# Sixteen expert blocks run inside the end of the first stage, on a row table read from the sort's sum of the first eight pairs

## Chip, core and metric

The kernel runs on one core of a Trainium2 chip. The metric is the device time of one launch in microseconds (us): 733.31 is the median of three runs of the kernel before (730.54 to 735.48).

## What is computed

`x` holds 32 sequences of 56 tokens of width 256; each sequence has a context of 1500 rows. Four steps follow one another, each added to the residual. The second one concerns the change: a mixture of 16 experts in which every token takes the 6 with the highest scores. The code below is shortened.

```python
x = x + xattn0(layernorm(x), ctx, ...)   # a decayed scan over ctx, averaged over its 1500 rows, then a norm
x = x + moe0(layernorm(x), ...)          # 16 experts, the best 6 per token
x = x + xattn1(layernorm(x), ctx, mask)  # softmax attention over the unmasked rows
x = x + moe1(layernorm(x), ...)          # 2 experts, the best 1

def moe0(h, gate_w, w_gate, w_up, w_down):          # h: 1792 x 256
    scores = softmax(h @ gate_w.T)                  # 1792 x 16
    topk_w, topk_idx = top_k(scores, 6)
    cw = zeros(1792, 16).at[rows, topk_idx].add(topk_w)
    y = 0
    for e in range(16):
        out = silu(h @ w_gate[e].T) * (h @ w_up[e].T) @ w_down[e].T   # inner width 176
        y = y + cw[:, e:e + 1] * out
    return y
```

## The kernel before

**Pairs.** Two sequences share one tile of 128 partitions, so there are 16 pairs (`NP`). PE, DVE, ACT and SP follow the order of the program as written (L90) throughout; POOL does so from the second stage on.

**First stage** (L234 to L767). A loop over the pairs (L643) streams the context through a ring of five slots of 1.5 MB (`slots`, `load_ctx`), sums it on TensorE (`count_in`, acc L325), forms the first residual, norms it (`first_norm`, `residual`, `second_norm`), writes the normed rows to DRAM (`away`, `xn0`) and scores the experts (`gate`, `best`). The pairs are staggered over the steps of the loop: pair p is normed one step after it is summed, ranked two after and sorted three after.

**Sorting tokens to experts.** `ranks` and `counted` give each chosen token its place in the queue of its expert (`pos`; `base0` is the running count). `places` splits this place into a level (place divided by 128, at most 14) and an offset. `ones_at` builds one-hot rows of the offsets, half of one of its two tiles on POOL. `sorted_in` (owned L593) multiplies and sums them into one PSUM bank, `owned`: for each expert and level, the 128 token numbers and their weights. It is summed over all 16 pairs in one go. A block is one level of one expert: 128 rows; the blocks are ordered by level, so that blocks 0 to 15 are the first 128 rows of each expert.

**The tail of the first stage** (L685 to L767) finishes pairs 13, 14 and 15, copies `owned` to SBUF, and picks out the rows of the used blocks (bl L750) into `idx` (row numbers), `wgt` (weights) and `ei` (which expert each block has). `busy` (d L583) issues matmuls on data that nothing reads. The weights of the 16 experts (`w0_sb`) come over SP's queue: the down weights in pieces (`w0_down_pieces`), the up weights at pair 13 (`load_w0_up`).

**Second stage**: `expert_blocks` over 95 blocks (`NB0`), written out in steps. In step t, TensorE does the gate and up product of block t (`gate_up`, gu L785), turns the hidden rows of block t-1 (`turn`, tp L803), turns the gathered rows of block t+1 (tp L195, copied by ACT L197) and does the down product of block t-2 (`down`, y L812). ACT applies silu (sg L791), DVE the product (hs L797). POOL gathers each block's rows by `idx` (xb L943), seven blocks ahead; the result goes to DRAM (`ys0`). `side(t)` hangs other work on step t: the windows of context for the third stage (`load_window`), the residual written out (`xr0`), the mask rows, and the gathers that add finished blocks back to the residual (`result`, L856).

**Third and fourth stage**: the attention, and the two experts over 15 blocks. After them a general path runs only if the flag `bad` is set (L1439).

Of the kernel before, what the change touches and what calls it, by code (L numbers as in the profile page):

```python
# [8 lines left out]
F32 = mybir.dt.float32  # L9
# [34 lines left out]
NB0 = NBW - E0 // 4  # L44
NY1 = 3
NB1 = B * S // P + 1
WP = 2 * D + 2
# [12 lines left out]
def xattn_ffn_kernel(  # L60
# [91 lines left out]
    starts = const.tile([1, B], I32, name="starts")  # L152
    bad = const.tile([1, 1], I32, name="bad")

    ring = const.tile([P, NRING, CW], F32, name="ring")
# [78 lines left out]
    with tc.tile_pool(name="p1", bufs=1) as p1, tc.tile_pool(name="p3", bufs=3) as p3, tc.tile_pool(  # L234
# [19 lines left out]
        bin_sb = p1.tile([P, KD], F32, name="bin_sb")  # L254
        bout_sb = p1.tile([1, D], F32, name="bout_sb")
        gam = p1.tile([P, D], F32, name="gam")
# [110 lines left out]
        PE.matmul(vp[:, 0:D], lhsT=ones[0:1, :], rhs=bout_sb, start=False, stop=True)  # L367
        cvec = p1.tile([1, D], F32, name="cvec")
        A.copy(cvec, vp[0:1, 0:D])
# [16 lines left out]
        for l in range(NL):  # L386
            G.memset(lev[:, l, :], float(l * P))
        iota = p1.tile([P, P], F32, name="iota")
# [189 lines left out]

        def busy(n):

            for _ in range(n):
                d = psa.tile([P, 512], F32, tag="acc", name="d")
                PE.matmul(  # L583
                    d, lhsT=ident, rhs=slots[B % NRING][:, 0:2, :].rearrange("p j d -> p (j d)"),
                    start=True, stop=True,
                )

        def sorted_in(p, h=None):

            t = pend[p]  # L590
            for e in range(E0) if h is None else range(NE * h, NE * h + NE):
                c, g = divmod(e, 4)
                PE.matmul(  # L593
                    owned[Q * g : Q * g + Q, c, :],
                    lhsT=vals[:, p % 2, e].rearrange("p o l -> p (o l)"),
                    rhs=t["hots"][e // NE][:, e % NE, :],
                    start=(p == 0 and c == 0), stop=(p == NP - 1 and c == 3),
                )
# [44 lines left out]
        for p in range(NP):  # L643
            if p >= 1:
                first_norm(p - 1)
            if p >= 3:
                ones_at(p - 3, 0)
            if p >= 1:
                residual(p - 1)
                count_in(2 * p)  # L650
                count_in(2 * p + 1)
            sum_out(p)
            if p >= 1:
                second_root(p - 1)
# [24 lines left out]
            if p % 2 == 0 and p + 2 < NP:  # L679
                first_rows(p + 2)  # L680
            if p == NP - 3:
                load_w0_up()
            if p > NP - 3:
                some_pieces(6)
        last = NP - 1  # L685
# [24 lines left out]

# [14 lines left out]
        for c in range(4):  # L725
# [43 lines left out]
    def expert_blocks(nb, nq, f, w, ei, wk, ptr, pgu, pht, py, rows_of, done, ahead, wgt=None, side=None, xT0=None):  # L769

# [3 lines left out]
        piece = doff + 2 * D  # L774
        units = [(i, u) for i in range(nb) for u in range(nq)]
        xT, at, hs, hT, y = {}, {}, {}, {}, {}
# [42 lines left out]

        xb = {i: rows_of(i) for i in range(min(ahead, nb))}  # L820
        xT[0] = xT0 or turned_rows(wk, ptr, "tr", xb[0])
        xb.pop(0)
        if side:
            side(-1)
        for t in range(len(units) + 2):
# [11 lines left out]
            if side:  # L837
                side(t)

# [88 lines left out]
    with tc.manual_schedule(  # L928
# [82 lines left out]
        def late_or_bad():  # L1011
# [7 lines left out]
            V.tensor_reduce(t8s[0:1, 0, 0:1], lp[0:1, 0:P], AX.X, ALU.max)  # L1019
            V.tensor_scalar(bad, t8s[0:1, 0, 0:1], 0.0, bad, ALU.is_gt, ALU.max)  # L1020
            V.tensor_scalar(
                bad, slot[0:1, NL - 1, E0 - 1 : E0], float(NB0), bad, ALU.is_gt, ALU.max
            )

        todo = [(blocks_by(p) + 4, p, k) for p in soon for k in range(K0)]
        sums = []
# [12 lines left out]
        def side(t):  # L1039
# [5 lines left out]
            if t > 1:  # L1045
                for _ in range(3):
                    if ways_:
                        next_ = ways_.pop(0)
                        next_()
            if 0 < t <= B // 2:  # L1050
                load_window(t - 1)
            if t == B // 2 + 1:
                nc.sync.dma_start(
                    out=xr0.rearrange("(p r) d -> r p d", r=P), in_=xr,
                )
            if 0 < t - B // 2 - 1 <= B:
                b = t - B // 2 - 2
# [33 lines left out]
            NB0, 1, F0, w0_sb.rearrange("p e w -> p (e w)"), ei,  # L1091
            wk, ptr, pgu, pht, py, rows_of, done, 7, wgt, side,
        )
# [590 lines left out]
```

## Time and profile before

The profiled execution took 731.96 us; its span, from the first to the last instruction, is 730.3 us with a mean granted TensorE clock of 0.954.

| stretch, us from the start of the span | what runs there |
|---|---|
| 0 to 186 | the loop over the pairs; a pair each 8.5 to 9.2 us at its end |
| 186 to 214 | the tail of the first stage, up to the first gate and up product |
| 214 to 464 | the 95 expert blocks |
| 464 to 559 | the attention |
| 559 to 730 | the last mixture |

| engine | busy us | share of the span |
|---|---|---|
| PE | 655.7 | 90% |
| DVE | 401.3 | 55% |
| ACT | 241.5 | 33% |
| POOL | 349.5 | 48% |

A busy share is an average over stages with different limits; the chain of waits, which is followed back from the last instruction, tells which engine an interval was waiting for. PEld is the load of a matmul's stationary operand, which runs beside PE; the granted clock is a share of TensorE's full speed.

### The profile page before, as it was taken

The page shows a single profiled execution, that of the slowest core. Times are in us where ns is not written, and L with a number is a line of the kernel's source. Part 1 is how long each engine was busy: PE and PEld are TensorE (multiplying, and loading weights), DVE is VectorE, ACT ScalarE, POOL GpSimd, SP SyncE. Part 2 cuts the span into 40 slices and gives each one's busy share as a digit, 9 for nine tenths or more (in the row PEclk, how much of TensorE's full clock was granted, in tenths as well). Part 3 has the DMA queues.
Part 4 walks back from the last instruction along what each step waited for, and adds up shares of the span by engine and source line. Part 5 has one row for each costly group of instructions (what it writes and reads, how often), then busy time and mean ns, then how long its engine had stood idle before and what let it go on. Part 6 is the DMA issues. An engine that isn't in the chain of part 4 may idle for free.

```text
span 730.3 us, 13508 instructions
## 1 busy us (share of the span) xinstructions
PE 655.7 (90%) x4099; PEld 438.6 (60%) x4099; DVE 401.3 (55%) x1378; ACT 241.5 (33%) x704; POOL 349.5 (48%) x440
## 2 busy tenths in 40 slices
PE   3558988888779999999999999999988999999996
PEld 3424555555447777667777776666654666666664
DVE  3578687878824655534454447677876232322322
ACT  0113233333214444444444443566551111111110
POOL 6265455554344357667776776568342202112111
PEclk9869799999669999999999999999999999999999
DMA  8969899999716899645554554695941201011000
GB/s 259 316 271 391 316 364 356 369 358 315 214 50 203 265 334 286 206 138 144 153 155 136 157 160 131 185 313 108 332 149 53 69 9 44 25 36 39 26 30 18
DMA packets 70656, 136.62 MB, mean 187 GB/s; under 512 B 7731, under 2 KB 43204, under 8 KB 70580
## 3 DMA queue, kind: packets, MB, share of 16 engines
q1 hardware_dynamic: 56036, 100.31, 39.9%
q0 software_dynamic: 14544, 35.37, 18.0%
q8 instruction: 38, 0.62, 0.4%
q14 instruction: 38, 0.31, 0.1%
HBM read 109.54 MB, written 26.77 MB: 187 GB/s over the span
## 4 chain that ended last, share of the span: by engine, by line
PE 77%; DVE 11%; ACT 3%; POOL 2%; issue 2%; DMA 1%; POOLq 0%; DVEq 0%
PE gu L785 29%; PE y L812 18%; PE acc L325 7%; PE tp L803 5%; PE tp L195 4%; PE tp L913 2%; PE sp L1142 2%; PE owned L593 2%; PE bp L467 1%; PE op L1177 1%; PE lp L505 1%; POOL xn L491 1%; PE sT L459 1%; DVE st L183 1%; ACT xT L197 1%
## 5 line engine op out<-in xcount | busy, mean ns | idle before, releaser
L785 PE MATMUL gu<-w_sb,xT 128*128 x380 | 130.8, 466 | 3.4 <-ACT xT L197 1.9
L791 ACT ACTIVATE sg<-gu 128x176 f32<-128x176 f32 (+1 forms) x155 | 53.1, 343 | 230.3 <-PE gu L785 227.9
L943 POOL DMA_INDIRECT xb<-xn,idx x95 | 91.2, 960 | 63.1 <-PE tp L195 39.7
L785 PE MATMUL gu<-ring,xT 128*128 x240 | 113.7, 597 | 0.0
L797 DVE SCALAR_TENSOR_TENSOR hs<-sg,wgt,gu 128x176 f32<-128x176 f32 x95 | 37.7, 397 | 119.8 <-ACT sg L791 119.8
L812 PE MATMUL y<-w_sb,hT 88*128 x380 | 97.9, 380 | 0.0
L785 PEld LDWEIGHTS gu<-w_sb,xT 128*128 128x128 f32 x380 | 71.5, 191 | 30.7 <-ACT xT L197 2.9
L856 POOL DMA_INDIRECT g<-ys,early x78 | 74.8, 959 | 29.1 <-issue 15.3
L795 DVE TENSOR_TENSOR hs<-sg,gu 128x256 f32<-128x256 f32 x60 | 25.2, 421 | 112.3 <-ACT sg L791 112.3
L1428 POOL DMA_INDIRECT out<-ob,ti x15 | 14.8, 989 | 126.8 <-DVE ob L1425 126.5
L803 PEld LDWEIGHTS tp<-ident,hs 128*88 128x88 f32 (+1 forms) x310 | 40.0, 129 | 57.9 <-issue 46.9
L812 PEld LDWEIGHTS y<-w_sb,hT 88*128 88x128 f32 x380 | 64.5, 190 | 5.7 <-issue 0.6
L785 PEld LDWEIGHTS gu<-ring,xT 128*128 128x128 f32 x240 | 45.6, 192 | 33.3 <-issue 30.4
L805 DVE COPY hT<-tp 88x256 f32<-88x256 f32 (+1 forms) x155 | 64.3, 415 | 0.2 <-PE tp L803 0.2
L812 PE MATMUL y<-ring,hT 128*128 x240 | 61.7, 380 | 0.0
L197 ACT COPY xT<-tp 128x256 f32<-128x256 f32 x126 | 46.9, 372 | 43.4 <-PE tp L195 35.3
L803 PE MATMUL tp<-ident,hs 128*88 128x128 f32 (+1 forms) x310 | 59.2, 273 | 0.0
L325 PE MATMUL acc<-ring,cz 128*32 128x256 f32 x768 | 54.7, 442 | 0.2 <-DVE cz L301 0.2
L951 ACT COPY yb<-y 128x256 f32<-128x256 f32 x95 | 35.3, 372 | 42.8 <-PE y L812 41.9
L432 POOL TENSOR_SCALAR z<-xr,mva,rsa 128x256 f32<-128x256 f32 x16 | 23.0, 1437 | 49.6 <-DVE xr L479 45.4
L195 PE MATMUL tp<-ident,xb 128*128 128x128 f32 x220 | 42.5, 275 | 2.4 <-issue 2.4
L812 PEld LDWEIGHTS y<-ring,hT 128*128 128x128 f32 x240 | 41.0, 190 | 3.3
(307 smaller groups left out, 996.7 us busy)
## 6 DMA issues: line engine op xcount, KB each, us to landing
ring<-in_cx SPq DMA_DIRECT2D x32, 1536.0 KB
ys<-yb SPq DMA_DIRECT2D x95, 128.0 KB
ring<-in_cx SPq DMA_DIRECT2D x16, 384.0 KB
extra<-in_cx SPq DMA_DIRECT2D x16, 384.0 KB
xs<-zrow SPq DMA_DIRECT2D x5, 771.0 KB
w_sb<-in_wg SPq DMA_DIRECT2D x2, 1408.0 KB
w_sb<-in_wu SPq DMA_DIRECT2D x2, 1408.0 KB
xn<-xn SPq DMA_DIRECT2D x16, 128.0 KB
```

The lines of the kernel that those rows point to most:

```text
L195: PE.transpose(tp[:, k * P : (k + 1) * P], xn[:, k * P : (k + 1) * P], ident)
L197: A.copy(xT.rearrange("p k c -> p (k c)"), tp[:, 0 : KD * P])
L325: PE.matmul(acc[Q * g : Q * g + Q, 0:D], lhsT=cz[:, j, 1 - h : 1 - h + Q], rhs=c[:, j, :], start=(h == 0 and m == 0), stop=(h == 1 and m = ...
L785: PE.matmul(gu[:, 0 : 2 * fp], lhsT=xT[i][:, k, :], rhs=w[:, bass.ds(at[i] + (u * piece + k * 2 * fp), 2 * fp)], start=(k == 0), stop=(k = ...
L791: A.activation(sg, gu[:, 0:fp], AF.Silu)
L797: V.scalar_tensor_tensor(hs[i, u], sg, wgt[:, i : i + 1], up, ALU.mult, ALU.mult)
L803: PE.transpose(tp[0:h, c * P : (c + 1) * P], a[:, c * h : (c + 1) * h], ident)
L805: V.tensor_copy(hT[i, u], tp[0:h, 0 : 2 * P])
L812: PE.matmul(y[i][:, 0:D], lhsT=a[:, c * P : (c + 1) * P], rhs=w[0:h, bass.ds(at[i] + (u * piece + doff + c * D), D)], start=(u == 0 and c ...
L856: G.indirect_dma_start(out=g, out_offset=None, in_=ys0[0 : n * P, :], in_offset=bass.IndirectOffsetOnAxis(ap=at[:, p, k : k + 1], axis=0),)
L943: G.indirect_dma_start(out=xb, out_offset=None, in_=xn0, in_offset=bass.IndirectOffsetOnAxis(ap=idx[:, i : i + 1], axis=0),)
L951: A.copy(yb, y[:, 0:D])
```

## The change

The sort's sum is cut in two: `owned` is summed over pairs 0 to 7, copied to `own0`, and started anew for pairs 8 to 15; at the end the two are added. From the first sum, `first_table` reads the first 128 rows of each expert, as row numbers `idx0` and weights `wgt0`. `soon_step` and its helpers run blocks 0 to 15 on these in 18 steps, placed among the instructions of the tail; the rows and results lie in ring slots that are free by then. The second stage starts at block 16. `busy` is taken out. If an expert had fewer than 128 rows after eight pairs and got more later, `lack` is positive and sets the flag `bad`. The windows, which go into the same ring slots, are loaded two per step in steps 16 to 23, and the residual is written out before block 16. The experts' up weights come in three parts. Copies by ACT stand in `soon_step` where `turn` uses DVE.

```diff
+PC = 8
...
-    def load_w0_up():
+    def load_w0_up(a, b):
         for m, w in ((0, wg0), (1, wu0)):
             for k in range(KD):
                 nc.sync.dma_start(
-                    out=w0_sb[:, :, (2 * k + m) * F0 : (2 * k + m + 1) * F0],
-                    in_=w[:, k, :].rearrange("p (e f) -> p e f", f=F0),
+                    out=w0_sb[:, a:b, (2 * k + m) * F0 : (2 * k + m + 1) * F0],
+                    in_=w[:, k, a * F0 : b * F0].rearrange("p (e f) -> p e f", f=F0),
                 )
...
+        def first_table():
+            V.tensor_scalar(cut, base0[0:1, :], float(P), None, ALU.min)
+            A.copy(own0.rearrange("p c r -> p (c r)"), owned.rearrange("p c r -> p (c r)"))
+            bl = ps.tile([P, 512], F32, tag="ps", name="bl")
+            for o in range(2):
+                for c in range(4):
+                    PE.matmul(
+                        bl[:, o * E0 + 4 * c : o * E0 + 4 * c + 4], lhsT=own0[:, c, :],
+                        rhs=ident.rearrange("p (g o l) -> p o l g", o=2, l=NLP)[:, o, 0, :],
+                        start=True, stop=True,
+                    )
+            V.tensor_copy(idx0, bl[:, 0:E0])
+            V.tensor_copy(wgt0, bl[:, E0 : 2 * E0])
...
-                    start=(p == 0 and c == 0), stop=(p == NP - 1 and c == 3),
+                    start=(p in (0, PC) and c == 0), stop=(p in (PC - 1, NP - 1) and c == 3),
...
                 sorted_in(p - 3)
+            if p - 3 == PC - 1:
+                first_table()
...
             if p == NP - 3:
-                load_w0_up()
+                load_w0_up(0, 4)
+                load_w0_up(4, 12)
             if p > NP - 3:
                 some_pieces(6)
+            if p == NP - 1:
+                some_pieces(len(pieces))
+                load_w0_up(12, E0)
...
+        def soon_rows(n):
+            for _ in range(n):
+                i = len(egot)
+                if i < E0:
+                    egot.append(i)
+                    G.indirect_dma_start(
+                        out=xbs[i], out_offset=None, in_=xn0[0 : PC * P, :],
+                        in_offset=bass.IndirectOffsetOnAxis(ap=idx0[:, i : i + 1], axis=0),
+                    )
...
+        def soon_turned(i):
+            tp = ps.tile([P, 512], F32, tag="ps", name="tp")
+            for k in range(KD):
+                PE.transpose(tp[:, k * P : (k + 1) * P], xbs[i][:, k * P : (k + 1) * P], ident)
...
+            A.copy(exT[i].rearrange("p k c -> p (k c)"), tp[:, 0:D])
+
+        def soon_step():
+            t = eat[0]
+            eat[0] += 1
+            if 0 <= t - 1 < E0:
...
+                A.activation(sg, gu[:, 0:F0], AF.Silu)
...
+                V.scalar_tensor_tensor(
+                    ehs[i], sg, wgt0[:, i : i + 1], gu[:, F0 : 2 * F0], ALU.mult, ALU.mult
+                )
+            if t < E0:
...
+                for k in range(KD):
+                    PE.matmul(
+                        egu[t][:, 0 : 2 * F0], lhsT=xT[:, k, :],
+                        rhs=w0_sb[:, t, 2 * k * F0 : 2 * (k + 1) * F0],
+                        start=(k == 0), stop=(k == KD - 1),
+                    )
+            if 0 <= t - 1 < E0:
...
+                for c in range(2):
+                    PE.transpose(tp[0:H0, c * P : (c + 1) * P], a[:, c * H0 : (c + 1) * H0], ident)
+                ehT[t - 1] = two_of("hT", D, D)[0:H0]
+                A.copy(ehT[t - 1], tp[0:H0, 0 : 2 * P])
+            if t + 1 < E0:
+                soon_turned(t + 1)
+            if 0 <= t - 2 < E0:
...
+                for c in range(2):
+                    o = 2 * KD * F0 + c * D
+                    PE.matmul(
+                        y[:, 0:D], lhsT=a[:, c * P : (c + 1) * P], rhs=w0_sb[0:H0, i, o : o + D],
+                        start=(c == 0), stop=(c == 1),
+                    )
+                yb = ybs[i % 8]
+                A.copy(yb, y[:, 0:D])
+                nc.sync.dma_start(out=ys0[i * P : (i + 1) * P, :], in_=yb)
+
         last = NP - 1
+        soon_rows(2)
         first_norm(last)
+        soon_turned(0)
         ones_at(NP - 3, 0)
         residual(last)
+        soon_rows(2)
         ones_at(NP - 3, 1)
         second_root(last)
         ranks(NP - 2)
         second_norm(last)
         away(last)
-        some_pieces(len(pieces))
+        soon_step()
+        soon_rows(2)
         sorted_in(NP - 3, 0)
         turned(last)
         sorted_in(NP - 3, 1)
         gate(last)
-        busy(1)
+        soon_step()
+        soon_rows(2)
         counted(NP - 2)
         places(NP - 2)
         best(last)
+        soon_step()
+        soon_rows(2)
         ranks(last)
         for h in range(2):
             ones_at(NP - 2, h)
+        soon_step()
+        soon_rows(2)
         for h in range(2):
             sorted_in(NP - 2, h)
         counted(last)
+        V.scalar_tensor_tensor(
+            lack, base0[0:1, :], float(P), cut, ALU.min, ALU.subtract
+        )
...
-        busy(1)
+        soon_step()
+        soon_rows(4)
         places(last)
         for h in range(2):
             ones_at(last, h)
+            soon_step()
...
+        soon_step()
         for h in range(2):
             sorted_in(last, h)
-        A.copy(own.rearrange("p c r -> p (c r)"), owned.rearrange("p c r -> p (c r)"))
+        V.tensor_tensor(own, owned, own0, ALU.add)
+        soon_step()
         bl = ps.tile([P, 512], F32, tag="ps", name="bl")
...
-        busy(2)
...
         V.tensor_copy(ei, ep[0:1, 0:P])
+        while eat[0] < E0 + 2:
+            soon_step()
...
-            if 0 < t <= B // 2:
-                load_window(t - 1)
-            if t == B // 2 + 1:
+            if t == E0 - 1:
                 nc.sync.dma_start(
                     out=xr0.rearrange("(p r) d -> r p d", r=P), in_=xr,
                 )
+            if 0 <= t - E0 < B // 4:
+                for h in range(2):
+                    load_window(2 * (t - E0) + h)
...
-        todo = [(blocks_by(p) + 4, p, k) for p in soon for k in range(K0)]
+        todo = [(max(blocks_by(p) + 4, E0 + 8), p, k) for p in soon for k in range(K0)]
```

More of the change, by code (lines that the diff above doesn't have):

```diff
@@ L153, in xattn_ffn_kernel @@
     bad = const.tile([1, 1], I32, name="bad")
+    lack = const.tile([1, E0], F32, name="lack")
     ring = const.tile([P, NRING, CW], F32, name="ring")
@@ L254, in xattn_ffn_kernel @@
         bin_sb = p1.tile([P, KD], F32, name="bin_sb")
-        bout_sb = p1.tile([1, D], F32, name="bout_sb")
+        bout_sb = pw0.tile([1, D], F32, name="bout_sb")
         gam = p1.tile([P, D], F32, name="gam")
@@ L367, in xattn_ffn_kernel @@
         PE.matmul(vp[:, 0:D], lhsT=ones[0:1, :], rhs=bout_sb, start=False, stop=True)
-        cvec = p1.tile([1, D], F32, name="cvec")
+        cvec = pw0.tile([1, D], F32, name="cvec")
         A.copy(cvec, vp[0:1, 0:D])
@@ L386, in xattn_ffn_kernel @@
         for l in range(NL):
-            G.memset(lev[:, l, :], float(l * P))
+            G.memset(lev[:, l, :], float(l * P) if l else -1.0)
         iota = p1.tile([P, P], F32, name="iota")
@@ L577, in ones_at @@
             pend[p].setdefault("hots", []).append(oh)
[L579 to L586, printed above, removed]
+        idx0 = p1.tile([P, E0], I32, name="idx0")
+        wgt0 = p1.tile([P, E0], F32, name="wgt0")
+        cut = p1.tile([1, E0], F32, name="cut")
+        own0 = p1.tile([P, 4, P], F32, name="own0")
+        def first_table():
[11 more added lines that the diff above has]
+            V.tensor_copy(wgt0, bl[:, E0 : 2 * E0])
         def sorted_in(p, h=None):
@@ L681, in xattn_ffn_kernel, with two_of @@
             if p == NP - 3:
-                load_w0_up()
+                load_w0_up(0, 4)
+                load_w0_up(4, 12)
             if p > NP - 3:
                 some_pieces(6)
+            if p == NP - 1:
+                some_pieces(len(pieces))
+                load_w0_up(12, E0)
+        rest = slots[B % NRING].rearrange("p j d -> p (j d)")[:, CW - 2 * (2 * F0 + 2 * D) :]
+        taken = {}
+        def two_of(name, o, n):
+            i = taken[name] = taken.get(name, 1) ^ 1
+            return rest[:, i * (2 * F0 + 2 * D) + o :][:, 0:n]
@@ new lines, in xattn_ffn_kernel @@
+        xbs = [slots[3][:, j, :] for j in range(NCH)] + [slots[4][:, j, :] for j in range(4)]
+        ybs = [slots[4][:, 4 + j, :] for j in range(8)]
+        exT, egu, ehs, ehT = {}, {}, {}, {}
+        def soon_rows(n):
[7 more added lines that the diff above has]
+                    )
@@ new lines, in xattn_ffn_kernel @@
+        egot, eat = [], [0]
+        def soon_turned(i):
+            tp = ps.tile([P, 512], F32, tag="ps", name="tp")
+            for k in range(KD):
+                PE.transpose(tp[:, k * P : (k + 1) * P], xbs[i][:, k * P : (k + 1) * P], ident)
+            exT[i] = two_of("xT", 0, D).rearrange("p (k c) -> p k c", k=KD)
+            A.copy(exT[i].rearrange("p k c -> p (k c)"), tp[:, 0:D])
[3 more added lines that the diff above has]
+            if 0 <= t - 1 < E0:
+                i = t - 1
+                gu = egu.pop(i)
+                sg = two_of("sg", 2 * D, F0)
+                A.activation(sg, gu[:, 0:F0], AF.Silu)
+                ehs[i] = two_of("hs", 2 * D + F0, F0)
+                V.scalar_tensor_tensor(
+                    ehs[i], sg, wgt0[:, i : i + 1], gu[:, F0 : 2 * F0], ALU.mult, ALU.mult
+                )
+            if t < E0:
+                egu[t] = psa.tile([P, 512], F32, tag="acc", name="gu")
+                xT = exT.pop(t)
+                for k in range(KD):
[5 more added lines that the diff above has]
+            if 0 <= t - 1 < E0:
+                tp = ps.tile([P, 512], F32, tag="ps", name="tp")
+                a = ehs.pop(t - 1)
+                for c in range(2):
[5 more added lines that the diff above has]
+            if 0 <= t - 2 < E0:
+                i = t - 2
+                y = ps.tile([P, 512], F32, tag="ps", name="y")
+                a = ehT.pop(i)
+                for c in range(2):
[7 more added lines that the diff above has]
+                nc.sync.dma_start(out=ys0[i * P : (i + 1) * P, :], in_=yb)
@@ L767, in xattn_ffn_kernel, with expert_blocks @@
         V.tensor_copy(ei, ep[0:1, 0:P])
-    def expert_blocks(nb, nq, f, w, ei, wk, ptr, pgu, pht, py, rows_of, done, ahead, wgt=None, side=None, xT0=None):
+        while eat[0] < E0 + 2:
+            soon_step()
+    def expert_blocks(nb, nq, f, w, ei, wk, ptr, pgu, pht, py, rows_of, done, ahead, wgt=None, side=None, xT0=None, first=0):
         fp = f // nq
@@ L774, in expert_blocks @@
         piece = doff + 2 * D
-        units = [(i, u) for i in range(nb) for u in range(nq)]
+        units = [(i, u) for i in range(first, nb) for u in range(nq)]
         xT, at, hs, hT, y = {}, {}, {}, {}, {}
@@ L818, in down @@
                 done(i, y.pop(i))
-        xb = {i: rows_of(i) for i in range(min(ahead, nb))}
-        xT[0] = xT0 or turned_rows(wk, ptr, "tr", xb[0])
-        xb.pop(0)
+        xb = {i: rows_of(i) for i in range(first, min(first + ahead, nb))}
+        xT[first] = xT0 or turned_rows(wk, ptr, "tr", xb[first])
+        xb.pop(first)
         if side:
-            side(-1)
+            side(first - 1)
         for t in range(len(units) + 2):
@@ L837, in expert_blocks @@
             if side:
-                side(t)
+                side(first + t)
     def levels_of(p):
@@ L1020, in late_or_bad @@
             V.tensor_scalar(bad, t8s[0:1, 0, 0:1], 0.0, bad, ALU.is_gt, ALU.max)
+            V.tensor_reduce(lack[:, 0:1], lack, AX.X, ALU.max)
+            V.tensor_scalar(bad, lack[:, 0:1], 0.0, bad, ALU.is_gt, ALU.max)
             V.tensor_scalar(
@@ L1091, in xattn_ffn_kernel @@
             NB0, 1, F0, w0_sb.rearrange("p e w -> p (e w)"), ei,
-            wk, ptr, pgu, pht, py, rows_of, done, 7, wgt, side,
+            wk, ptr, pgu, pht, py, rows_of, done, 7, wgt, side, None, E0,
         )
```

## The prediction

> **What bounds the kernel now.** I read the page first, then the chain of waits from 130 to 260 us, then the busy time by stretches, then single rows of the timeline.
>
> ```profile
> PE 77%; DVE 11%; ACT 3%; POOL 2%; issue 2%; DMA 1%; POOLq 0%; DVEq 0%
> ```
>
> This line of the page says that most of the end time follows from TensorE. Where it does is in the chain (start, length, what):
>
> ```profile
> 141.49 2.77 PE acc L325 x48
> 150.69 4.42 PE acc L325 x48
> ...
> 192.04 1.01 PE owned L593 x16
> 193.06 0.97 PE lp L505 x4
> 194.02 1.89 PE d L583 x2
> ...
> 210.74 2.41 DMA xb<-xn,idx
> ...
> 213.93 2.68 PE gu L785 x4
> ...
> 253.27 1.19 PE gu L785 x4
> ...
> 255.76 1.19 PE gu L785 x4
> ```
>
> From 213.93 (block 0) to 255.76 (block 16) every step is TensorE's; the pitch is 255.76 - 253.27 = 2.49 us: 1.19 gate and up, 0.22 and 0.22 transposes, 0.87 down. Before 213.93 there is a tail of serial steps, padded with `busy` (d), ending in a gather that nothing covers. The stretches show how TensorE fares there (columns: stretch, length, busy of PE, PEld, DVE, ACT, POOL, granted clock, DMA share, GB/s):
>
> ```profile
> 188.50:192.00 3.50, 1.73 (x22) 0.98 (x22) 3.13 (x12) 0.50 (x2) 0.00 (x0) 0.50 0.62 174
> 192.00:198.00 6.00, 5.93 (x55) 4.36 (x58) 4.85 (x18) 1.45 (x5) 2.40 (x4) 0.50 0.48 142
> 198.00:205.50 7.50, 6.31 (x54) 3.77 (x46) 6.66 (x17) 0.90 (x3) 0.63 (x2) 0.50 0.24 70
> 255.80:300.00 44.20, 44.20 (x215) 33.37 (x214) 23.19 (x90) 18.96 (x54) 28.32 (x31) 1.00 0.93 304
> ```
>
> From 188.5 to 205.5 the clock is half, though TensorE counts as 80 to 99% busy from 192 on; the blocks run at full clock without a gap, with the DMA at 0.93. Two more rows are needed, ACT's table change and the time from a gather's issue to its landing while the DMA is loaded (255 to 300):
>
> ```profile
> 213.52 1.28 ACT L791 ACT_TABLE_LOAD   x1
> DMA to landing us min/median/max: 3.7/4.9/5.8
> ```
>
> **What is removed.** Blocks 0 to 15 leave the second stage: 255.76 - 213.93 = 41.8 us, of which 16 x 2.49 = 39.8 is work that comes back in the tail, and 2.0 the slow start. The dummy matmuls (1.89 + 2.00 + 0.88 on the chain) go too, as does the open gather. What counts is when TensorE starts block 16, so I walk the new tail from 186.4, where the last pair's norm begins.
>
> **To the last pair's transpose.** POOL is free at 182.47 + 1.23 = 183.7; the first early gather lands 4.9 later, at 188.8 (bounds 3.7 to 5.8). TensorE's queue holds the first early transpose ahead of pair 14's ranks, so it stands until then, as it stood from 187.1 to 188.7 before; the clock falls to half as before. At half clock: transpose 0.64, ranks 0.45 + 0.59, gate and up of block 0 2.27 (the row at 217.50), transpose 0.64, half of pair 13's sort 1.08, the last pair's transpose 0.69: 195.2, where before it ended at 192.04.
>
> **The first silu.** ACT copies the turned rows (0.37), changes its table (1.28, the row above) and does silu (0.32); DVE's product takes 0.40: 197.6. This product stands in DVE's queue ahead of pair 14's `counted` and `places`, which began at 191.22 before. They take 2.2 (199.8), then ACT's two small steps 0.51 + 0.17 (200.5), then `best` 0.93: the last pair's choice is known at 201.5 instead of 195.2.
>
> **The table goes back and forth.** `best` uses exp, the next early step silu. After 200.5: load 1.28, exp 0.31 + 0.19, load 1.28, silu 0.32, product 0.40, with gaps 204.5. TensorE has done block 2's gate and up by 201 and waits for this product, with the last pair's ranks queued behind it: a hole of over 3 us. Then the rest of that step 1.31, ranks 0.40, a full step 2.49, pair 14's sort 1.0 make 5.2; for the hole I charge one more spell at half clock. The clock changes at 188.5, 205.5, 212.4 and 219.4, multiples of some 3.45; such a spell loses 1.7. So 211.4. The levels' column (0.53 DVE, 0.39 ACT, eight matmuls 0.93 at full clock) ends at 213.3, against 201.55.
>
> **The dense part.** Four early steps 9.9, 0.5 for a product that stands behind a 1.19 us one-hot row on DVE, the last pair's sort 1.0, one more step 2.5, which hides the new addition of two sums (512 columns: between 0.39 for 224 and 0.95 for 760), row picking 2.02 and 0.11: `idx` at 229.3, against 208.2. Nine steps remain; two have no gate and up: 7 x 2.49 - 0.22 + 1.96 = 19.1, so 248.5. They cover the first gather of the second stage (landing 4.9). A transpose 0.44, ACT's copy 0.37 and gaps: block 16 starts at 249.4, 6.3 earlier than 255.76. The drained pipeline has 1.96 less to do in the next two steps, and stands twice 0.44 for the copy of turned rows as at 216.6: 1.1 more. Together 7.4.
>
> **The rest.** `first_table` is 16 instructions at 2.02/16, so 2.0, and waits for ACT's 0.58 copy, of which TensorE's idle 0.66 before the next transpose takes most. The first context sum that then matters is that at 150.69: it took 4.42 instead of 2.77, waiting for data, which covers 1.65. I charge 0.5 (0 to 2.2, the latter if that wait is gone). POOL's 16 gathers (1.25 each with the gap) pass in front of its one-hot rows: pair 13's are done at 191.1 for a use at 194.5 or later, pair 14's at 201.0 for a use at 210: nothing; without that cover up to 2.4. SP issues the same bytes of weights in another order, done at 196 as before, and pair 15's rows stay behind them; the first three quarters of the up weights go ahead, so block 0 doesn't wait (if it waited for all, up to 6.5). ACT gets 16 x (0.32 + 3 x 0.37) = 22.9 us and DVE 6.4, into engines that were busy 7.8 and 19.2 of the 37 us from 185 to 222. In steps 16 to 23 two windows, a write and a gather make 1.0 MB per 2.49 us, over the 304 GB/s of the row above; gathers are seven blocks (17 us) ahead, so I charge nothing (0 to 3 if they come late). Result gathers of pairs 0 and 1 move from step 20 to 24 and join the next group: POOL has two gathers, 2.48, per step of 2.49: nothing (0 to 1).
>
> Sum: 7.4 - 0.5 = 6.9 us, from 731.96 to 725.1. That execution lay 1.35 below the median of 733.31, so as a median 726.4. The terms' bounds (gather -1.2 to +0.9, table spells, clock 0 to 3.4 in all, the rest 0 to 6 against) make a gain of 0 to 10.
>
> **A rule on the tables.** In "ScalarE: Activation LUTs", section "What ACT_TABLE_LOAD costs", the Trainium skill counts a drain of 1.38 us beside the 1.28 of the load for each change of set, and its section on table sets says to batch calls by set: this speaks against the change. The trace shows 1.28 and no drain: the copy before the load ended at 213.50, two hundredths ahead of it. By the page three waited loads would cost 4.1 more, and the gain would be 2.8.
>
> **A rule on the clock.** "TensorE: Matmul & The Clock Gate", Part 1, has the full clock come after one busy window of about 3.4 us. The second stretch above shows 5.93 of 6.00 us busy and a clock of 0.50, and the release came 7.5 us later. By the page the spell charged at 205.5 would be over sooner and the sum up to 1.7 better.
>
> **Rivals.**
>
> *TensorE alone sets the tail.* If the table loads fall into time in which ACT and TensorE have other work and the clock is full, then from 188.8 the tail is 39.8 of blocks and 7.9 of the tail's own (ranks 0.8, sorts 3.0, transpose 0.4, scores 0.6, the rest 3.1), 0.9 to restart: block 16 at 237.4, a gain of 18.4 + 1.1 - 0.5 = 19, 713 us. For it: ACT was busy only those 7.8 of 37 us. Against it: the order on DVE and ACT is fixed, and silu, exp, silu stand in it. Chance of getting half of the way or more (gain 10 to 19): 0.22.
>
> *The clock stays half in the tail.* Place: from 205.5 on, after the hole. Each 3.45 us spell at half costs 1.7, so four beyond the one charged, to about 223, turn the sum into a loss. For it: five such spells in a row stand in the trace, with TensorE mostly busy. Against it: early steps are wide matmuls, and 212.4 to 219.4 shows such matmuls winning the clock back within 7 us. Until `idx` it would cost 18.5: 734 to 744 us. Chance 0.13.
>
> *The flag is set*, so that the general path runs too: 16 x 16 blocks, about 256 x 2.49 = 637 us more. Against it: eight pairs hold 896 tokens, 6/16 of which are 336 per expert, where 128 are needed. Chance 0.02.
>
> **Chances.** The walk (gain 0 to 10) has 0.58; 0.05 is left for stalls that I haven't seen. One per cent (7.3 us) is about what a measurement can tell from no change. The walk's 6.9 lies just inside: of its 0.58 I put 0.20 above, 0.38 inside. Faster by over 1%: 0.20 + 0.22 = 0.42. Within: 0.38 + 0.04 of the clock's case = 0.42. Slower: 0.16. The range, 714 to 739, reaches from near the fast rival's end to the middle of the clock's; the walk's own is 723 to 733.
>
> **What would show it.** Right: block 16 starting near 249; two more table loads near 196 and 201 to 203; TensorE waiting for a product (hs) about 3 us before a transpose of hidden rows; ranks of the last pair near 206 and `idx` near 229; 79 blocks at 2.49 after it. Wrong: a first early gather landing after 190, a clock of 0.5 after 210, TensorE waiting for the weights' DMA, or holes in steps 16 to 30.

## The result, and the profile after

| kernel | median us | lowest to highest | ratio, 95% interval |
|---|---|---|---|
| before | 732.87 | 730.54 to 735.48 | |
| changed | 768.89 | 768.04 to 771.57 | 1.0497 [1.0452, 1.0542] |

The change costs 36.0 us. The profiled execution took 768.04 us with a span of 766.3, also 36.0 more than before (730.3). Line numbers below are those of the changed kernel or of the experiment named. The last line of the page on the chain of waits has TensorE ending 63% of the span now, instead of 77%:

```profile
PE 63%; DVE 5%; ACT 2%; issue 1%; DMA 1%; POOL 1%; POOLq 0%; ACTq 0%; DVEq 0%
```

Starts of the same pieces of work in both timelines show where the time went. "Sum 10" is pair 10's first context sum, "last norm" the last pair's addition (z) that opens the walk of the prediction; block 19 is the first that runs at the steady pitch of 2.49 us in both:

| start, us | sum 1 | sum 10 | sum 14 | last norm | `idx` | block 19 | end |
|---|---|---|---|---|---|---|---|
| before | 45.88 | 132.23 | 168.85 | 186.36 | 208.19 | 263.06 | 730.3 |
| changed | 53.24 | 138.06 | 180.57 | 220.31 | 262.95 | 297.44 | 766.3 |
| later by | 7.4 | 5.8 | 11.7 | 34.0 | | 34.4 | 36.0 |

So 34 of the 36 us are lost ahead of the tail in which the early blocks run. Three stalls make them: 5.8 up to sum 10, 5.9 from there to sum 14, 22.2 from sum 14 to the last norm. The tail itself, from last norm to block 19, takes as long as before (77.1 against 76.7), where the prediction had it 7.4 shorter.

**The start.** POOL's timeline of the changed kernel, then of the one before (start, length, line, operation; in brackets the idle time ahead and what ended it):

```profile
29.85 0.51 POOL L374 DMA_DIRECT2D sm<-cvec  x1 [15.25 <-ACT cvec L371]
35.83 0.77 POOL L389 MEMSET lev<- 128x16 f32 x14 [5.47 <-issue]
```
```profile
27.41 0.65 POOL L387 MEMSET lev<- 128x16 f32 x14 [13.61 <-issue]
28.60 0.51 POOL L372 DMA_DIRECT2D sm<-cvec  x1 [0.55 <-DMA ring<-in_cx]
```

Before, `lev` was written first. Now `cvec` lies in pool `pw0` (a pool is a stretch of on-chip memory; when it closes, later tiles get its space), and `lev` is in the space that follows it: it has to wait until the copy of `cvec` to `sm` has landed, 5.9 us after its issue. DVE's first pieces in that space wait as well (L396 at 36.07; before, L394 at 28.98).

**The early table.** TensorE's timeline of the changed kernel:

```profile
145.33 2.45 PE L593 MATMUL bl<-ident,own 128*128 128x4 f32 x16 [0.80 <-ACT own L589]
...
150.88 5.35 PE L327 MATMUL acc<-ring,cz 128*32 128x256 f32 x48
```

0.80 of waiting for ACT's copy and 2.45 of matmuls, and then the context sum takes 5.35 us, not 2.80: the clock has fallen to half, as this stretch shows (columns as in the prediction):

```profile
148.00:156.20 8.20, 7.74 (x57) 3.64 (x55) 6.35 (x25) 1.84 (x7) 3.61 (x5) 0.50 0.35 110
```

The kernel before has a slow sum two steps after sum 10, too, the one of 4.42 at 150.69. It did not wait for data: TensorE was busy throughout, at half clock.

```profile
151.10:154.30 3.20, 3.20 (x36) 1.61 (x32) 3.03 (x7) 0.57 (x3) 0.00 (x0) 0.50 0.74 276
```

**POOL.** The chain of waits of the changed kernel through the last pairs, the stretches around it, and the same norm (xn) in POOL's timeline of the kernel before:

```profile
203.49 0.95 POOL ring L721
204.48 1.25 POOL xn L493
205.78 0.70 PE tp L197 x2
...
209.11 5.28 PE acc L327 x48
```
```profile
181.00:190.00 9.00, 6.42 (x88) 3.82 (x80) 6.81 (x21) 1.85 (x8) 7.40 (x9) 1.00 1.11 323
190.00:200.00 10.00, 0.00 (x0) 0.00 (x0) 0.00 (x0) 0.00 (x0) 7.56 (x9) 0.55 1.00 293
200.00:209.00 9.00, 2.76 (x8) 1.72 (x8) 0.67 (x6) 1.28 (x5) 7.10 (x9) 0.50 0.36 107
```
```profile
173.97 1.24 POOL L491 TENSOR_SCALAR xn<-xr,mv 128x256 f32<-128x256 f32 x1 [4.54 <-ACT mv L190]
```

For ten microseconds nothing runs but POOL, and what POOL runs is the early gathers (ring L721): all 16 stand ahead of the norm of pair 13 (xn L493), 13 of them in one row, and TensorE's transpose of these rows waits for it. The norm starts 23.9 us after sum 14, before the change 5.1: 18.8 of the 22.2. The other 3.4 come behind the hole, where the transposes, the scores and sum 15 (5.28 instead of 2.77) run at a clock of 0.50. In the written order no gather stands there: the first two follow the loop's last step. But in the first stage POOL does not follow the written order, and the scheduler, which then chooses POOL's order when the program is built, put them all in front.

**The tail.** The same chain, further on:

```profile
226.70 1.28 ACT L743
228.00 0.33 ACT ring L743
...
231.97 1.28 ACT L527
...
233.66 1.28 ACT L743
234.96 0.33 ACT ring L743
235.31 0.41 DVE ring L745
235.76 0.66 PE tp L761 x2
...
284.68 1.54 issue
286.22 0.42 PE tp L197 x2
...
288.07 2.71 PE gu L897 x4
...
291.67 2.28 PE gu L897 x4
...
294.85 1.45 PE gu L897 x4
```

The three table loads and the hole before the transpose of hidden rows are there as forecast. Not forecast are the last lines: TensorE stands before block 16, and its clock has to come back. POOL's timeline tells why:

```profile
282.17 0.53 POOL L1050 MEMSET zrow<- 128x514 f32 x1 [49.65 <-issue]
...
283.00 1.04 POOL L1055 DMA_INDIRECT xb<-xn,idx  x1 [0.15 <-issue]
```

`idx` was ready at 263, but `zrow` is written 0.1 us after the last early product (DVE, 281.7 to 282.1), which reads `wgt0`: `zrow` lies in that tile's space, and the gathers are queued behind it.

### The profile page after: what moved, and what is told of

The parts are those of the page before. It is cut to its first block, busy times and chain, and to the rows that moved or that the text cites. A ratio compares the mean times of both kernels' runs of the same rounds, so it can differ in the third digit from the quotient of the medians.

```text
span 766.3 us, 13426 instructions
## 1 busy us (share of the span) xinstructions
PE 663.3 (87%) x4107; PEld 439.8 (57%) x4107; DVE 397.3 (52%) x1369; ACT 247.0 (32%) x722; POOL 351.3 (46%) x440
## 4 chain that ended last, share of the span: by engine, by line
PE 63%; DVE 5%; ACT 2%; issue 1%; DMA 1%; POOL 1%; POOLq 0%; ACTq 0%; DVEq 0%
PE gu L897 25%; PE y L924 15%; PE tp L915 4%; PE tp L197 3%; PE gu L752 2%; PE tp L1025 2%; PE y L772 2%; PE sp L1257 2%; PE op L1292 2%; PE tp L761 1%; PE acc L327 1%; PE tp L1014 1%; PE sp L1251 1%; PE owned L606 0%; PE tp L1284 0%
## 5 line engine op out<-in xcount | busy, mean ns | idle before, releaser
L897 PE MATMUL gu<-w_sb,xT 128*128 x316 | 109.3, 468 | 3.7 <-ACT xT L199 2.4
L1055 POOL DMA_INDIRECT xb<-xn,idx x79 | 76.0, 961 | 29.0 <-issue 9.9
L924 PE MATMUL y<-w_sb,hT 88*128 x316 | 81.4, 380 | 0.0
L909 DVE SCALAR_TENSOR_TENSOR hs<-sg,wgt,gu 128x176 f32<-128x176 f32 x79 | 31.4, 397 | 89.9 <-ACT sg L903 89.9
L897 PEld LDWEIGHTS gu<-w_sb,xT 128*128 128x128 f32 x316 | 59.4, 192 | 26.5 <-ACT xT L199 3.2
L327 PE MATMUL acc<-ring,cz 128*32 128x256 f32 x768 | 61.1, 482 | 0.3 <-DVE cz L303 0.3
L917 DVE COPY hT<-tp 88x256 f32<-88x256 f32 (+1 forms) x139 | 57.7, 415 | 0.2 <-PE tp L915 0.2
L924 PEld LDWEIGHTS y<-w_sb,hT 88*128 88x128 f32 x316 | 53.6, 190 | 4.9 <-issue 0.6
L327 PEld LDWEIGHTS acc<-ring,cz 128*32 128x32 f32 x768 | 30.1, 136 | 28.6 <-issue 17.8
L578 POOL TENSOR_SCALAR oh<-iota,off 128x128 f32<-128x128 f32 x60 | 35.7, 609 | 17.9 <-DVE off L554 14.1
```

What stands on the lines that cost most here:

```text
L327: PE.matmul(acc[Q * g : Q * g + Q, 0:D], lhsT=cz[:, j, 1 - h : 1 - h + Q], rhs=c[:, j, :], start=(h == 0 and m == 0), stop=(h == 1 and m = ...
L578: G.tensor_scalar(oh[:, i, :], iota, off[:, i : i + 1], None, ALU.is_equal)
L897: PE.matmul(gu[:, 0 : 2 * fp], lhsT=xT[i][:, k, :], rhs=w[:, bass.ds(at[i] + (u * piece + k * 2 * fp), 2 * fp)], start=(k == 0), stop=(k = ...
L909: V.scalar_tensor_tensor(hs[i, u], sg, wgt[:, i : i + 1], up, ALU.mult, ALU.mult)
L917: V.tensor_copy(hT[i, u], tp[0:h, 0 : 2 * P])
L924: PE.matmul(y[i][:, 0:D], lhsT=a[:, c * P : (c + 1) * P], rhs=w[0:h, bass.ds(at[i] + (u * piece + doff + c * D), D)], start=(u == 0 and c ...
```

## The experiments

The sets ran on several chips. On one of them the kernel before took 731.6, on the other four 775 to 780; there ACT, DVE and POOL stood 13 to 38 us in each profile at waits that end with "remote", which no profile from the chips with 732 has. Ratios compare with the kernel before on the same chip. 1% is 7.8 us on the slower chips.

**Set 1 (before: 779.48): one cause at a time.** POOL in written order, from ahead of the loop over the pairs (`x1_pool`); `cvec` over weights that arrive later (`x2_cvec`); both, and the early table in the pool that stays open (`x3_three`):

```diff
+        p1x.enter_context(
+            tc.manual_schedule(engines={ET.PE, ET.DVE, ET.Activation, ET.SP, ET.Pool})
+        )
         for p in range(NP):
```
```diff
-        cvec = pw0.tile([1, D], F32, name="cvec")
+        cvec = w0_sb[0:1, 12, 0:D]
```
```diff
+    idx0 = const.tile([P, E0], I32, name="idx0")
+    wgt0 = const.tile([P, E0], F32, name="wgt0")
...
-        idx0 = p1.tile([P, E0], I32, name="idx0")
-        wgt0 = p1.tile([P, E0], F32, name="wgt0")
```

> The changed kernel with POOL, too, in written order from the loop over the pairs on, so that the 16 early gathers stand in the tail where they are written, and not ahead of pair 13's normed rows. Theory (the gathers' place in POOL's queue costs the loop): the 17.1 us that TensorE waited for those rows go, and the half clock behind it: 20 to 24 us less than the changed kernel, 745 to 749 us. Rival (the loop waits there for data or for SP): within 3 us of 769.

> The changed kernel with the vector cvec in a free corner of the weights' space in place of the pool that is closed at the start. Theory (POOL's and DVE's first writes into that pool's space wait for the small transfer that reads cvec): POOL's memsets of the levels start near 28 us again in place of 35.8, the first pairs' loop 7 us earlier; 5 to 8 us less than the changed kernel, 761 to 764. Rival (the loop is bound by the context's transfer, so that the start's delay is made up): under 2 us.

> The changed kernel with three things undone: POOL in written order, cvec as above, and the early table (row numbers and weights) in the space that stays for the whole kernel, so that the second stage's first tiles do not take its place. Theory (three separate delays that add up: 22, 6, and 4 for the second stage's gathers issued 19 us before block 16 rather than after the last early product): 769 - 32 = 737, between 733 and 741, what is left over the kernel before being the first table in the loop. Rival (the early blocks themselves cost the tail more than they save): over 745.

The kernel before with only the two tiles moved, as the change moves them (`b1_cvec`):

```diff
-        bout_sb = p1.tile([1, D], F32, name="bout_sb")
+        bout_sb = pw0.tile([1, D], F32, name="bout_sb")
...
-        cvec = p1.tile([1, D], F32, name="cvec")
+        cvec = pw0.tile([1, D], F32, name="cvec")
```

> The kernel before with only the output bias and cvec moved into the pool that is closed at the start, as the change does. Theory: 5 to 8 us slower than the kernel before, 738 to 741, with POOL's memsets of the levels near 36 us. Rival (made up later in the loop): within 2 us of 733.

Ratios: 1.0448 [1.0353, 1.0543], 1.0412 [1.0333, 1.0492], 1.0242 [1.0170, 1.0314], and 1.0128 [1.0051, 1.0205] for `b1_cvec`. The times in the first three expectations can't be compared with a chip of 780. The starts in the first stage can: with POOL's order the last norm comes at 194.8, with `cvec` moved at 204.9, with all three at 189.3, against 220.3. (With `cvec` moved, the start gives back 6.1 at sum 1; besides, POOL's timeline has only ten gathers ahead of pair 13's norm there, and sum 14 to the last norm takes 32.91 instead of 39.74.) `b1_cvec` has sum 1 at 52.75 (45.88 before) and its `lev` at 35.34: the move alone makes the start's stall, and its last norm is still 6.9 later (193.27).

**Set 2 (before: 775.45).** The changed kernel itself; with only the early table in the pool that stays open (`z1_space`, third diff above); `x3_three` with the early table's matmuls two steps later (`y0_table`); and that with three edits in the tail (`y1_tail`):

```diff
+                if p == PC + 4:
+                    first_rows_of()
                 count_in(2 * p)
...
+            if p == NP - 1:
+                soon_rows(3)
             if p >= 1:
                 second_norm(p - 1)
...
         gate(last)
-        soon_step()
         soon_rows(2)
...
-                A.copy(ehT[t - 1], tp[0:H0, 0 : 2 * P])
+                (V.tensor_copy if late else A.copy)(ehT[t - 1], tp[0:H0, 0 : 2 * P])
...
         while eat[0] < E0 + 2:
-            soon_step()
+            soon_step(True)
```

> The changed kernel once more, beside its variants on the chip of this call, so that starts and ends can be compared on one chip. If the chip of the runs before this one was slow for all kernels in the second stage, the ratio to the kernel before stays at 1.05 wherever it runs, and the first context sum of pair 15, the last norm and block 16 start within 1 us of 209.0, 220.3 and 288.1. If the change itself loses more where gathers land late, the ratio is above 1.06 on such a chip.

> The changed kernel with idx0 and wgt0 in the pool that stays open, so that POOL's memset of zrow need not wait for the last early product. Theory: the gathers of the second stage are issued right after the row table, near 263 instead of 283, and block 16 follows the last early step at 285 without an idle gap and at full clock: 4 to 7 us below the changed kernel (762 to 765, or a ratio to the kernel before of 1.040 to 1.044). Rival: the gathers wait for another reason (the weights' load, the ring slot): within 1 us of the changed kernel and block 16 at 288.

> The kernel with the three parts (POOL's written order, cvec over weights that the first step no longer needs, the early table in the pool that stays open), and the sixteen matmuls of the early table two steps later, ahead of context sums that waited 1.65 us for their data. Theory: the step from pair 10 to pair 11 falls from 11.1 to some 9.5 us, the following one keeps its clock, and pair 14's first sum comes at 169 to 170 instead of 171.8; 2 to 3 us below the kernel with three parts. Rival: the clock falls to half wherever these narrow matmuls stand, and nothing is gained.

> As the kernel with the moved table, and in the tail: three early gathers ahead of pair 14's second norm on POOL (TensorE waited 2.3 us for the first of them), no early step between the last pair's scores and its choice (silu then follows exp once, one table load instead of three; TensorE waited 4.25 us there), and the hidden rows' copy by DVE in the steps after the row table (pitch 2.49 instead of 2.62). Theory: 2.3 + 3 + 1 + 9 x 0.13 = 7 us below the kernel with the moved table, so within 1 per cent of the kernel before if the second stage runs as on the first chip, and 1 to 2 per cent above if gathers land late there. Rival: the removed step must run later anyway, and at full clock: 3 us or less.

Ratios: 1.0603 [1.0547, 1.0658], 1.0554 [1.0507, 1.0600], 1.0268 [1.0207, 1.0329], 1.0297 [1.0257, 1.0337]. The changed kernel loses 1% more on this chip, at the edge of the second case of its expectation (above 1.06), though its last norm starts at 218.7. `z1_space` is 3.8 us better, with overlapping intervals, and misses its range, so its time decides nothing; what the gathers wait for is read from its timelines of POOL and of TensorE:

```profile
261.94 0.53 POOL L1050 MEMSET zrow<- 128x514 f32 x1 [29.16 <-issue]
...
266.46 1.03 POOL L1055 DMA_INDIRECT xb<-xn,idx  x1 [3.84 <-PE ep L874]
```
```profile
292.25 1.45 PE L897 MATMUL gu<-w_sb,xT 128*128 x4 [0.58 <-ACT xT L201]
...
294.38 1.45 PE L897 MATMUL gu<-w_sb,xT 128*128 x4 [0.46 <-ACT xT L201]
```

The gathers now follow `idx`, and blocks 16 and 17 run at full clock, 2.13 us apart (3.60 in the changed kernel). Block 16 itself is no earlier, 72.5 us after the last norm against 71.2 in `after_again`, as TensorE stands 2.14 us for a copy by ACT at 278.29. `y0_table` missed: the step that the table left got shorter (8.7 us), but the step that it went to took 14.1, at half clock. Its premise was wrong, too: the slow sum there had not waited for data (151.10 above). `y1_tail` was no better than `y0_table`, against its theory.

**Set 3 (before: 731.56, 31 runs).** The kernel before with the sort's sum in two, the early table and the addition, without early steps (`b2_table`: `first_table` as in the change, `cvec` as in `x2_cvec`), and with POOL's written order from the loop on (`b4_pool`: first diff above); `x3_three` with that order only from the loop's last step on (`x5_late`); and `x5_late` with the edits of `y1_tail` and an early table of half as many matmuls (`y3`):

```diff
         for p in range(NP):
+            if p == NP - 1:
+                p1x.enter_context(
+                    tc.manual_schedule(
+                        engines={ET.PE, ET.DVE, ET.Activation, ET.SP, ET.Pool}
+                    )
+                )
```
```diff
-            for o in range(2):
-                for c in range(4):
-                    PE.matmul(
-                        bl[:, o * E0 + 4 * c : o * E0 + 4 * c + 4], lhsT=own0[:, c, :],
-                        rhs=ident.rearrange("p (g o l) -> p o l g", o=2, l=NLP)[:, o, 0, :],
-                        start=True, stop=True,
-                    )
+            for c in range(4):
+                PE.matmul(
+                    bl[:, 8 * c : 8 * c + 8], lhsT=own0[:, c, :],
+                    rhs=ident.rearrange("p (go l) -> p l go", l=NLP)[:, 0, :],
+                    start=True, stop=True,
+                )
```

> The kernel before, with the sort's sum cut in two, the early table built after pair 7's sort, and the two sums added at the end; no early steps (bout_sb and cvec lie where they cost no wait). Theory: 0.5 to 2 us for sixteen narrow matmuls, plus one or two spells of half clock behind them as the changed kernel showed (its steps from pair 10 to 14 took 5.9 us more than before): 3 to 6 us slower, ratio 1.004 to 1.008. Rival, the forecast's own sizing: 0.5 us, within 0.3 per cent of the kernel before.

> The kernel before, with POOL following the order of the program as written from the loop over the pairs on, as the variants of the changed kernel with POOL's written order do. If that order costs nothing by itself: ratio within 0.3 per cent of 1. Rival: in the loop it puts pairs' instructions in another order on POOL (the norms of two pairs side by side), and that costs 2 to 8 us, which then also stands in those variants (ratio 1.003 to 1.010).

> The kernel with the three parts (POOL's written order, cvec over weights not needed yet, the early table in the pool that stays open), but POOL's written order begins only with the loop's last step, so that its order in the loop is that of the kernel before. If the written order in the loop cost something, this is 2 to 8 us below the kernel with three parts, whose ratio was 1.024: 1.014 to 1.021. Otherwise 1.024 again, within 0.004.

> As the last, with the early table read by four matmuls in place of eight, two steps later; three early gathers ahead of pair 14's second norm on POOL; no early step between the last pair's scores and its choice; the hidden rows' copy by DVE after the row table. Theory: each of these takes 1 to 3 us out, 5 to 8 in all below the version before it: ratio 1.006 to 1.012 on a chip of the slow kind, about 1.00 on the first one. Rival: the removed step only moves behind the row table and half clock eats the rest: ratio 1.02.

| kernel | median us | ratio, 95% interval | sum 10 | sum 14 | last norm | `idx` | block 19 |
|---|---|---|---|---|---|---|---|
| b2_table | 737.69 | 1.0064 [1.0040, 1.0088] | 132.52 | 174.12 | 191.64 | 215.30 | |
| b4_pool | 736.05 | 1.0074 [1.0047, 1.0102] | 130.09 | 169.51 | 187.02 | 209.56 | |
| x5_late | 736.51 | 1.0066 [1.0044, 1.0088] | 133.33 | 173.46 | 190.99 | 234.69 | 264.57 |
| y3 | 728.77 | 0.9963 [0.9944, 0.9982] | 134.17 | 172.47 | 189.99 | 226.00 | 258.93 |

The table alone costs 4.7 us in time (0.0064 x 731.56) and 5.0 from sum 10 to sum 14 (41.60 against 36.62); from the last norm to `idx` it loses 1.8 more, which no run takes apart. TensorE's timeline of `b2_table` has the changed kernel's wait and matmuls, and a slow sum:

```profile
139.78 2.35 PE L601 MATMUL bl<-ident,own 128*128 128x4 f32 x16 [0.80 <-ACT own L597]
...
145.25 4.12 PE L326 MATMUL acc<-ring,cz 128*32 128x256 f32 x48
```

`b4_pool` is slower by 5.4 us, as its rival said, so the kernels of sets 1 and 2 with this order may pay that too; its profiled execution (span 730.1) doesn't show where. With three small edits, none of which touches the early steps, `x5_late` loses 5 us where the change loses 36. `y3` is faster than the kernel before, by 1.3 to 4.1 us at the ends of its interval.

**Sets 4 and 5 (before: 779.73 and 775.23).** POOL's order from the last step on alone (`w1_pool`), with `cvec` (`w3_two`), and `x5_late` with the tail's edits but the table left in place (`w4_tail`); then three kernels again. The edits are those above.

> The changed kernel with POOL in the written order from the loop's last step on, and nothing else. Theory: the stall before pair 15's transpose (17.1 us) is this order's alone, so 20 to 22 of the 36 us go: ratio 1.019 to 1.023. Rival: what is behind POOL's gathers only moves into the tail, where the sort waits as long for its rows: ratio above 1.035.

> As the last, and cvec over weights that are not needed yet. Theory: the 6 to 7.4 us of the start go too: ratio 1.010 to 1.014. Rival: pair 12's late data or the half clock takes them back before the tail: less than 3 us gained. The difference to the kernel with all three parts (1.0066) is then what the gathers of the second stage cost when they wait for the last early product: 3 to 5 us.

> The kernel with the three parts and the changes of the tail (three early gathers ahead of pair 14's second norm, no early step between scores and choice, the hidden rows' copy by DVE after the row table), with the early table's sixteen matmuls where the change put them. If the tail is what made the last version faster than the kernel before: 730 to 732, ratio 0.998 to 1.001, and the moved table is worth the 1 to 3 us that remain. Rival: the moved table is worth 5 us or more: ratio 1.003 or above.

> The changed kernel with POOL in the written order from the loop's last step on, a second time, for a chip on which the kernel before takes some 732. There, theory: ratio 1.019 to 1.023, as 20 to 22 of the 36 us are POOL's order. Rival: above 1.035, the order's cost only moves. On a chip where it takes 780: 1.035 again within 0.006.

> The three parts and the tail's changes, with the early table where the change put it, a second time. On a chip of 732: 730 to 732 (ratio 0.998 to 1.001) if the tail made the faster version; 1.003 or above if the moved table did. On a chip of 780: 1.0235 again within 0.004.

> The version with the moved table of four matmuls, a second time. On a chip of 732: ratio 0.9963 again within 0.003. On a chip of 780: if its lead over the kernel before needs a chip on which ACT's short steps don't stand, it loses there as the others do, 1.015 to 1.025; if the lead holds on any chip, below 1.000.

Ratios: `w1_pool` 1.0349 [1.0284, 1.0414] and 1.0307 [1.0233, 1.0380]; `w3_two` 1.0254 [1.0178, 1.0331]; `w4_tail` 1.0235 [1.0203, 1.0266] and 1.0150 [1.0103, 1.0196]; `y3` 1.0156 [1.0099, 1.0213]. Against 1.0603, POOL's order takes 20 to 23 us out (0.0254 and 0.0296 of 778), on chips of the slower kind, though not the same chip. The ranges of `w1_pool` and `w3_two` (1.019 to 1.023 and 1.010 to 1.014) rested on losses measured on a chip of 732 and were missed here. Both runs of `w1_pool` go from sum 14 to the last norm in 17.51 us, to the hundredth what the kernel before needs; the changed kernel needs 39.74. POOL's timeline in the second of them:

```profile
190.71 1.24 POOL L493 TENSOR_SCALAR xn<-xr,mv 128x256 f32<-128x256 f32 x1 [4.53 <-ACT mv L192]
192.12 1.32 POOL L727 DMA_INDIRECT ring<-xn,idx  x1 [0.17 <-issue]
...
196.27 1.35 POOL L727 DMA_INDIRECT ring<-xn,idx  x1 [0.30 <-issue]
197.67 2.60 POOL L578 TENSOR_SCALAR oh<-iota,off 128x128 f32<-128x128 f32 x4
```

Pair 14's norm stands ahead of the first gather, four gathers ahead of the one-hot rows. `w4_tail_b` has sums 1 and 10 at 45.88 and 132.23, exactly as before, so moving `cvec` clears the start (sum 1 lies between 45.77 and 47.35 in all kernels with this edit). Whether the moved table or the tail made `y3` faster stays open: `w4_tail_b` and `y3_b` are equal here, and `w4_tail` has no run on a chip of 732.

And `y3` loses 1.6% on such a chip. Its ACT timeline in set 5 has a wait that its run in set 3 lacks:

```profile
194.59 0.37 ACT L201 COPY xT<-tp 128x256 f32<-128x256 f32 x1 [6.14 <-remote]
```

It lies ahead of the last norm (197.24, instead of 189.99), on a copy that the kernel before makes too. What "remote" is, the profile says no nearer than "another core or an unknown queue", and no run isolates it. That such waits cost the early steps more, as these hang on ACT's short copies and silus, is a guess: the kernel before has no profile from such a chip.

## Why the prediction was wrong, step by step

It said 726.4 and within or below a per cent; the time went up by 5%.

- **"POOL's 16 gathers ... pass in front of its one-hot rows ... nothing; without that cover up to 2.4."** This failed most. It took POOL's order for the written one, two gathers at a time, though the kernel's description says that POOL follows it only from the second stage on. In fact all 16 (1.25 each, 20.0) and four one-hot rows stood ahead of pair 13's norm, a row that the forecast did not look at: the norm came 18.8 late, the half clock behind the hole added 3.4. Together 22.2 where the forecast had nothing, and gone in `w1_pool`.
- **`first_table` at 0.5 (0 to 2.2).** Mis-sized: 5.0. The cover that it named does not exist. It read the sum of 4.42 at 150.69 as waiting for data; but that was the half clock (0.50 from 151.1 to 154.3, TensorE busy throughout). In `b2_table` that sum takes 2.80, and the one after it, at 164.45, takes 4.41: the slow spell has moved, not gone. The wait for ACT (0.80) was not hidden either, and the half clock behind the matmuls made the changed kernel's next sum 5.35 instead of 2.80; the prediction had charged spells of half clock in the tail only.
- **The move of `bout_sb` and `cvec`** had no price at all. It cost 5.8 to 6.9. `b1_cvec` has two tiles going into a pool that closes; what took that space next, here `lev` and DVE's pieces, had to wait for their last reader, a DMA of 5.9.
- **"They cover the first gather of the second stage."** Wrong in the changed kernel: the gathers were queued behind `zrow`, and that waited for the space of the early table. From `idx` to block 19 it takes 34.5, in `x5_late`, where nothing waits, 29.9: 4.6 us.
- **The walk of the tail** came out right up to `idx`, 42.9 us after the last norm, measured 42.6, in `x5_late` 43.7, but partly by luck. In the changed kernel the early rows had long landed, so that the forecast wait for them fell away. In `x5_late`, where it is there (it ends 1.9 after the last norm, forecast 2.4; 183.7 + 4.9 is 188.6, not 188.8), the last pair's transpose ends after 6.9 instead of 8.8, as the clock is half for one spell only (193.5 to 196.9). The hole is 4.37 (forecast over 3), and from its end to the end of pair 14's sort it takes 8.7 instead of 6.9, at half clock for two spells (0.50 from 207.2 to 214.0), where one was charged. The nine last steps took 21.3 instead of 19.1: the pitch is 2.62, as the transposes of the hidden rows wait for DVE's product, whose silu stands behind ACT's copy of y, and the drain waits 1.1 for a product. ACT's copy of the hidden rows is not what lengthens the pitch: in `y3`, where DVE makes it, the pitch is 2.68.
- **The restart, 1.1 less**: 0.4 in `x5_late`. With the steps above, the tail that nothing disturbs is 3.1 us shorter than before (73.6 against 76.7), not 7.4. A walk with no mistake but these would have said 5.0 - 3.1, a loss of 2; `x5_late` lost 5, of which 1.1 stood at sum 10 already.
- **The rest** (SP, windows, result gathers) at 0 to 6: 1.6 from block 19 on, right.
- **The rivals.** Neither TensorE alone nor the flag came; the clock was half in places of the tail, but not to `idx`. None had the mechanism that decided, an engine whose order is not the written one.

On tables, the Trainium skill ("ScalarE: Activation LUTs", "What ACT_TABLE_LOAD costs") adds a drain of 1.38 us to each load; in the chain above the load of 226.70 ends at 227.98 and silu starts at 228.00, so none is seen here. Its advice to batch by set (section "Table sets: the hidden batching unit") holds: in `y3`, where one load is left, the hole is 2.40 instead of 4.37.

## What to carry to other kernels

Before pricing a moved instruction, find out who orders its engine: where a scheduler does, it can put all of a group in front, and the price is the group's length, not that of two. A tile that changes its pool carries a wait to whoever takes its space next; list the last reader of each, DMAs among them. And check that an operation that takes long was waiting, by the busy time and the clock of its stretch, before its length is used as cover. A gain of a few us is soon eaten by such side costs: here the early blocks were worth 3 us in a tail that nothing disturbed (`x5_late`), and what came with them cost 34.

## What was not expected of the hardware

Sixteen matmuls of four columns cost about as much by the clock behind them as by their length: in the changed kernel 2.55 us on the next sum against 2.45. In `y0_table`, where the clock was at half before they began (0.50 from 147.0 to 150.4), stretches of TensorE's full busy time at half clock (columns as above):

```profile
151.00:154.00 3.00, 3.00 (x15) 3.00 (x15) 2.79 (x7) 0.50 (x2) 0.00 (x0) 0.50 0.35 121
154.00:159.00 5.00, 5.00 (x49) 2.17 (x49) 0.60 (x4) 0.00 (x0) 0.00 (x0) 0.50 0.21 34
```

TensorE counts as busy for 8 us, yet the clock stays at 0.50; in the first line PEld, the load of operands, is as busy as PE. The Trainium skill ("TensorE: Matmul & The Clock Gate", Part 1) has one busy window of about 3.4 us release the clock. The rows would agree if loads with hardly any columns behind them don't count as activity; that was not tried apart.
